# A layout change at the store side of a pairwise bilinear kernel: output rows 64 bytes longer in memory

## The chip, the cores and the metric

The kernel runs on one core of one Trainium2 chip. The metric is the device time of one launch in microseconds (us). Times of several runs are given as their median; a profile is one further execution, recorded by the hardware profiler, and its span runs from the first to the last instruction.

## The reference: what is computed

```python
# r_x: (4096, 32, 64) float32, W: (64, 64) float32
vid = jnp.einsum('bfd,de->bfe', x, W)
idx_i, idx_j = jnp.triu_indices(32, k=1)      # 496 pairs i < j
return x[:, idx_i, :] * vid[:, idx_j, :]      # (4096, 496, 64) float32
```

For each of 4096 samples, each of the 32 fields is multiplied by one 64x64 matrix, and then every pair of fields (i < j) gives one elementwise product. The input is 33.6 MB and the output 520 MB, so the kernel writes about fifteen times what it reads.

## The kernel before, in words

**Layout.** The host lays the input out transposed: 128 rows, one for each SBUF partition, where a row stands for one of the 64 embedding elements of one of two halves of the batch. Along a row, the data is cut into units of C = 128 float32 numbers, 512 B each: one unit holds one field (or one output pair) for 128 samples. The batch makes NT = 16 tiles of 256 samples (128 in each half). The output in memory is laid out in the same way, as 128 rows; each row holds 16 x 496 units of products, one tile after the other, and then PAD = 24 units that nobody writes or reads. A row is thus 7,960 units or 4,075,520 B long, which is 995 x 4,096 B. The host undoes this layout after the launch and drops the padding.

**Work.** For each tile, eight matmuls on TensorE (L172) multiply the 32 fields by a block-diagonal copy of W and leave `vid` in PSUM. VectorE then forms the 496 products with `tensor_tensor` (L196), reading x from SBUF and `vid` from PSUM by broadcast or strided views, in the order that `by_block` and `products` give. Everything in SBUF is one big tile `mem` of 445 units a partition. The products go into 70 slots in it, listed by hand in `SLOTS` with length and place, and the x tiles go to places listed in `XPLACE`, so that loads, products and stores share the memory as it comes free.

**Transfers.** All transfers are issued by SyncE (SP) in program order, and the order of SP and VectorE is the program's own. As soon as a slot is full, SP issues its store (L199): 128 partitions, and of each one a contiguous run of up to 127 units (65,024 B). The places in a row follow from `STARTS`: slot k is written to units `begin` to `end`, next to where slot k-1 ended. There are 70 stores. The 11 loads (L136, L140, L153) bring the first tile with W, then the other tiles in three groups. The first load of the program begins 256 B into a row of its array (`C - D` = 64 numbers), since W's 64 columns stand there.

The changed lines are the store at L199 and the host's declaration of the output array.

Of the kernel before, what the change touches and what calls it, by code (L numbers as in the profile page):

```python
# [14 lines left out]
C = 128  # L15
# [25 lines left out]


PAD = 24
PAD0 = 7


# [6 lines left out]
def by_block():  # L53


    def within(lo):
        yield "step", lo, 2, 1, 0
        for k in range(2):
            yield "step", lo, 4, 2, k
        for i in (lo, lo + 8):  # L60
            yield "row", i + 4, i, 4, 4
        yield "row", lo + 8, lo, 8, 8

    yield from within(0)
    yield "row", 16, 0, 16, 16
    yield from within(16)


def products(blocks, at=0):

    for kind, a, b, c, d in blocks:
        if kind == "row":
            rows, n, i0, di, j0, dj = c, d, b, 0, a, 1
        else:
            rows, n, i0, di, j0, dj = 16 // b, c, a, b, a + c + d, b
        r = k = 0
        while r < rows:
            room = BREAKS[bisect_right(BREAKS, at)] - at
            if k or room < n:
                m, w = 1, min(n - k, room)  # L80
            else:
                m, w = min(rows - r, room // n), n
            yield at, m, w, i0 + r * di + k, di, j0 + r * dj, dj
            at += m * w
            if k + w == n:
                r, k = r + m, 0
            else:
                k += w
# [10 lines left out]
@with_exitstack  # L99
def pairwise_bilinear_kernel(  # L100
    ctx: ExitStack,
    tc: tile.TileContext,
    x0: bass.AP,
    x: bass.AP,
    out: bass.AP,
):

    nc = tc.nc
    NT = sum(len(tiles) for group in GROUPS for tiles in group)
    F = x0.shape[1] - 1 - PAD0
    D = P // 2
    NP = F * (F - 1) // 2

    BANK = 512 // C


    ctx.enter_context(tc.manual_schedule(engines={mybir.EngineType.SP, mybir.EngineType.DVE}))

    const = ctx.enter_context(tc.tile_pool(name="const", bufs=1))
    psum = ctx.enter_context(
        tc.tile_pool(name="ps", bufs=1, space=bass.MemoryType.PSUM)
    )
    vid = psum.tile([P, F, C], F32)

    mem = const.tile([P, UNITS, C], F32)


    w2 = const.tile([P, P], F32)


    place = XPLACE[0]
    nc.sync.dma_start(  # L136
        out=mem.rearrange("p u c -> p (u c)")[:, place * C - D : (place + F // 2) * C],
        in_=x0.rearrange("p u c -> p (u c)")[:, C - D : (1 + F // 2) * C],
    )
    nc.sync.dma_start(out=mem[:, place + F // 2 : place + F, :], in_=x0[:, 1 + F // 2 : 1 + F, :])  # L140
    nc.vector.memset(w2, 0.0)  # L141
    for half in (slice(0, D), slice(D, P)):
        nc.vector.tensor_copy(w2[half, half], mem[half, place - 1, C - D :])  # L143
    loaded = 1

    def load(tiles, cuts=()):
        nonlocal loaded
        n = len(tiles) * F
        place = XPLACE[tiles[0]]
        at = (loaded - 1) * F  # L150
        loaded += len(tiles)
        return [
            nc.sync.dma_start(out=mem[:, place + lo : place + hi, :], in_=x[:, at + lo : at + hi, :])  # L153
            for lo, hi in cuts or [(0, n)]
        ]

    ready = mybir.DependencyInfo(mybir.DependencyClass.Sync, mybir.DependencyReason.DATA)

    def behind(later, earlier):
        tc.add_manual_dep(later.ins, earlier.ins.name, ready, reason="issued when that has landed")  # L160

    pieces = []
    groups, cuts = iter(GROUPS), iter(CUTS)
    for tiles, parts in zip(next(groups)[1:], next(cuts)):
        pieces = load(tiles, parts)

    for t in range(NT):
        xt = mem[:, XPLACE[t] : XPLACE[t] + F, :]


        for b in range(0, F, BANK):
            nc.tensor.matmul(  # L172
                vid[:, b : b + BANK, :],
                lhsT=w2,
                rhs=xt[:, b : b + BANK, :],
                start=True,
                stop=True,
            )

        for at, m, w, i, di, j, dj in products(by_block(), t * NP):  # L180
            slot = bisect_right(STARTS, at) - 1
            n = m * w
            begin, end = STARTS[slot], STARTS[slot + 1]
            ot = mem[:, SLOTS[slot][1] : SLOTS[slot][1] + SLOTS[slot][0], :]
            o = ot[:, at - begin : at - begin + n, :]
            if m == 1:
                left = xt[:, i : i + w, :]
                right = vid[:, j : j + 1, :].to_broadcast([P, w, C])
            else:
                o = o.rearrange("p (m w) c -> p m w c", m=m)  # L190
                right = vid[:, j : j + (m - 1) * dj + 1 : dj, :].unsqueeze(2).to_broadcast([P, m, w, C])
                if di == 0:
                    left = xt[:, i : i + w, :].unsqueeze(1).to_broadcast([P, m, w, C])
                else:
                    left = xt.rearrange("p (m d) c -> p m d c", d=di)[:, i // di : i // di + m, i % di : i % di + w, :]
            nc.vector.tensor_tensor(o, left, right, ALU.mult)  # L196
            at += n
            if at == end:
                store = nc.sync.dma_start(out=out[:, begin:end, :], in_=ot)  # L199
                if pieces:  # L200
                    behind(store, pieces[-2])
                    pieces.clear()


        if t + 2 == loaded < NT:
            (tiles,) = next(groups)
            pieces = load(tiles, next(cuts))
# [45 lines left out]
```

## Time and profile before

| | |
|---|---|
| median of 3 runs | 1287.49 us (1287.32 to 1287.50) |
| the profiled execution | 1287.45 us, of which the span is 1285.6 us |
| TensorE matmul busy | 230.2 us, 256 instructions |
| VectorE busy | 1084.0 us, 348 instructions |
| DMA, queue of the kernel's transfers | 11,664 packets, 553.69 MB, 99.8% of 16 engines' span |
| HBM read and written | 33.59 MB and 520.09 MB |

A packet is one record of a DMA engine: one contiguous run that it moved, or one semaphore update of 4 B at the end of its share of a transfer. 81 transfers of 128 rows make 10,368 runs, and 81 x 16 engines make 1,296 semaphore updates, which together are the 11,664 packets of the queue. The share of 16 engines' span says how much of the time the engines were occupied with packets. The trace holds each packet's start, duration and size.

### The profile page before, as it was taken

The numbers are of one execution on the slowest core, as the hardware profiler recorded it, in microseconds if no ns is written. First come the engines' busy times: TensorE is split into PE (matmuls) and PEld (weight loads), VectorE is DVE, ScalarE is ACT, GpSimd is POOL, SyncE is SP. The second block draws the span as 40 slices with busy tenths as digits, with TensorE's granted clock in tenths as the row PEclk, the third lists the DMA queues.
The fourth block names the chain that finished last, engine by engine and source line by source line (L and its number), as shares of the span: only waits on it lengthen the run. The fifth ranks groups of instructions, "written<-read, shape, count | busy, mean of one in ns | idle before, by whom it ended". The sixth has DMA issues, their size and how long they took to land.

```text
span 1285.6 us, 1143 instructions
## 1 busy us (share of the span) xinstructions
PE 230.2 (18%) x256; PEld 66.9 (5%) x256; DVE 1084.0 (84%) x348; POOL 0.2 (0%) x4
## 2 busy tenths in 40 slices
PE   4031221303120112040311211103122130312000
PEld 1000000100000000010000000000000000000000
DVE  6899998999967389899799992849998889999952
POOL 0000000000000000000000000000000000000000
PEclk8555565556555556555555555555556555555555
DMA  9999999999999999999999999999999999999998
GB/s 415 417 440 440 441 414 449 420 442 416 445 430 439 418 420 435 434 440 429 441 427 449 429 427 438 417 440 421 440 432 443 437 422 440 427 447 422 436 443 364
DMA packets 11670, 553.75 MB, mean 431 GB/s; under 512 B 1296, under 2 KB 1296, under 8 KB 1680
## 3 DMA queue, kind: packets, MB, share of 16 engines
q1 hardware_dynamic: 11664, 553.69, 99.8%
q8 instruction: 2, 0.03, 0.0%
q14 instruction: 4, 0.03, 0.0%
HBM read 33.59 MB, written 520.09 MB: 431 GB/s over the span
## 4 chain that ended last, share of the span: by engine, by line
DMA 46%; DVE 45%; issue 6%; DVEq 0%; SPq 0%
DVE mem L196 45%; DMA out_dram<-mem 41%; DMA mem<-in_r_x_dram 5%; DVEq L241 0%; SPq L153 0%; DVEq L196 0%; SPq L140 0%; SPq L136 0%; SPq L199 0%
## 5 line engine op out<-in xcount | busy, mean ns | idle before, releaser
L196 DVE TENSOR_TENSOR mem<-mem,vid 128x1024 f32<-128x1024 f32 (+17 forms) x345 | 1083.4, 3212 | 170.6 <-DMA out_dram<-mem 164.6
L172 PE MATMUL vid<-mem,w 128*128 128x512 f32 x256 | 230.2, 1034 | 952.8 <-DVE mem L196 885.0
L172 PEld LDWEIGHTS vid<-mem,w 128*128 128x128 f32 x256 | 66.9, 303 | 1114.5 <-DVE mem L196 1013.1
L143 DVE COPY w<-mem 64x64 f32<-64x64 f32 x2 | 0.4, 190 | 5.0 <-DMA mem<-in_r_x_dram 5.0
L141 DVE MEMSET w<- 128x128 f32 x1 | 0.2, 165 | 0.8 <-PEq L221 0.8
L221 POOL MEMSET const-bfloat16-1.0<- 128x1 bf16 x1 | 0.1, 101 | 0.0
L221 POOL MEMSET const-uint8-127<- 128x1 uint8 x1 | 0.1, 101 | 0.0
L221 POOL MEMSET const-float32-0.0<- 128x1 f32 x1 | 0.1, 98 | 0.2 <-issue 0.2
L221 POOL MEMSET const-float32-1.0<- 128x1 f32 x1 | 0.1, 98 | 0.0
## 6 DMA issues: line engine op xcount, KB each, us to landing
out_dram<-mem SPq DMA_DIRECT2D x15, 8128.0 KB, 27.5
out_dram<-mem SPq DMA_DIRECT2D x14, 7680.0 KB, 24.9
out_dram<-mem SPq DMA_DIRECT2D x6, 7168.0 KB, 26.2
out_dram<-mem SPq DMA_DIRECT2D x5, 7936.0 KB, 28.1
out_dram<-mem SPq DMA_DIRECT2D x3, 7424.0 KB, 22.6
out_dram<-mem SPq DMA_DIRECT2D x3, 5888.0 KB, 20.9
mem<-in_r_x_dram SPq DMA_DIRECT2D x2, 8128.0 KB, 37.9
out_dram<-mem SPq DMA_DIRECT2D x2, 8064.0 KB, 24.3
```

What stands on the lines that cost most here:

```text
L141: nc.vector.memset(w2, 0.0)
L143: nc.vector.tensor_copy(w2[half, half], mem[half, place - 1, C - D :])
L172: nc.tensor.matmul(vid[:, b : b + BANK, :], lhsT=w2, rhs=xt[:, b : b + BANK, :], start=True, stop=True,)
L196: nc.vector.tensor_tensor(o, left, right, ALU.mult)
L221: nc = _bacc.Bacc("TRN2", target_bir_lowering=False, num_devices=1, dynamic_dma_scratch_size=512)
```

## The change

Each row of the output in memory becomes 16 float32 numbers (`SHIFT`, 64 B) longer than before. Row p therefore begins 64 x p bytes later than it did. To allow a row length that isn't a whole number of units, the output is declared with two dimensions instead of three, and the store names its place in numbers instead of units. The loads, the products, the slots and the order of all instructions are as before: the instruction lists of the two programs have the same 70 stores of the same shapes, with the same waits, in the same places.

```diff
 PAD = 24
+SHIFT = 16
 PAD0 = 7
...
             if at == end:
-                store = nc.sync.dma_start(out=out[:, begin:end, :], in_=ot)
+                store = nc.sync.dma_start(out=out[:, begin * C : end * C], in_=ot.rearrange("p u c -> p (u c)"))
...
-        laid = (2 * D, NT * shape[1] + PAD, C)
+        laid = (2 * D, (NT * shape[1] + PAD) * C + SHIFT)
...
-    got = r.results[0]["out_0_dram"][:, : NT * NP].reshape(2, D, NT, NP, C)
+    got = r.results[0]["out_0_dram"][:, : NT * NP * C].reshape(2, D, NT, NP, C)
```

A row is now 4,075,584 B long. Before, every run of every store began and ended at a multiple of 512 B from the start of the array. Now 16 of the 128 rows (p a multiple of 8) still do; 32 (p a multiple of 4) begin at multiples of 256 B; 96 begin 64, 128 or 192 B past one. The SBUF side of each store is as it was.

## The prediction

> **What bounds the kernel now.** I read the engine table and the 40 slices first, then the queue table, then the waits of VectorE and of SP's queue, and then single packets. The first view is the page's engine line and its slices:
>
> ```profile
> PE 230.2 (18%) x256; PEld 66.9 (5%) x256; DVE 1084.0 (84%) x348; POOL 0.2 (0%) x4
> ...
> DMA  9999999999999999999999999999999999999998
> GB/s 415 417 440 440 441 414 449 420 442 416 445 430 439 418 420 435 434 440 429 441 427 449 429 427 438 417 440 421 440 432 443 437 422 440 427 447 422 436 443 364
> ```
>
> No compute engine fills the span, and the DMA digits stand at 9 in all slices but the last. The GB/s vary because a packet counts where it ends. The queue table says how full "9 or more" is:
>
> ```profile
> q1 hardware_dynamic: 11664, 553.69, 99.8%
> ...
> HBM read 33.59 MB, written 520.09 MB: 431 GB/s over the span
> ```
>
> The engines are occupied 99.8% of the span. The waits confirm who sets the pace. The two fences are the waits of VectorE and the waits of SP's queue (for what, us in total, times, longest):
>
> ```profile
> DVE mem L196 <- DMA out_dram<-mem: 164.6, 33, 21.6
> ```
>
> ```profile
> SPq L199 <- DVE mem L196: 1101.6, 66, 32.4
> ...
> SPq L241 <- DMA out_dram<-mem: 23.8, 1, 23.8
> ```
>
> VectorE is idle 164.6 us because a slot's old contents were still being stored. SP waits for VectorE too, 1101.6 us, but that starves nothing: a store takes 24.9 us (median) from issue to landing and 16 engines need about 17 us for its 7.43 MB (520.09 MB / 70 at 431 GB/s), so the next one is issued while the last one runs. In the packet records at least 16 packets are under way in 1275 of the 1285.6 us. The chain of waits changes hands between VectorE (45%) and the stores (41%), so neither view alone names a bound; what VectorE's 1084 us leave room for and the transfers don't decides it.
>
> So the time is the sum of the packets' durations over 16 engines, and a store packet's duration is the one thing that this change can touch. The steady part shows how regular they are (queue table of the stretch from 1000 to 1250 us):
>
> ```profile
> q1 hardware_dynamic: 1945, 108.40, 100.1%
> ```
>
> 108.40 MB in 1.001 x 16 x 250 us is 27.07 GB/s for one engine. The packet records say the same: the 65,024 B packets take 2399 ns in the median (2401.9 mean), the 61,440 B ones 2267 ns, the 8,192 B ones 309 ns, the 3,584 B ones 140 ns. A line through the first and the last of these is 27.20 GB/s plus 8.2 ns a packet. A semaphore update, 4 B, takes 9 ns.
>
> **The budget.** 553.7 MB / 16 engines / 27.20 GB/s is 1272.3 us. 10,368 / 16 = 648 runs an engine, at 8.2 ns, are 5.3 us. 81 updates an engine, at 9 ns, are 0.7 us. That makes 1278.3 us. All packet durations together, over 16, are 1282.9 us, so some 4.6 us lie above the line; 4.0 us of that are packets longer than the median of their own size. They come mostly where loads and stores run together: 62 KB stores that begin at 413 us take 2815 to 3342 ns instead of 2286 ns, and 13 KB loads after 440 us up to 1192 instead of 498. The other 2.7 us of the span are the start before the first packet and the end. Outside the span lie 1287.45 - 1285.6 = 1.85 us. The profiled execution is 0.04 us off the median of 1287.49 us, so its sum stands for the median.
>
> **The change part by part.** The declaration, the two-dimensional view and the host's slice change no instruction: 70 stores of the same shapes with the same waits, 256 matmuls and 345 products stay. I cost them at nothing, because a run is already the whole contiguous part of a row (65,024 B in one packet). If the two-dimensional view changed how a row is cut, the packet count of 11,664 would tell, and each additional cut would cost an engine 8.2 ns.
>
> Loads don't change either. What changes is the destination address of 8,960 store runs, 560 an engine. There are two effects to price.
>
> First, the odd start and end. A run that begins 64 B past a 256 B boundary has a short piece at its head and one at its tail. No operation of the trace before writes at such an address, so I bound it. From below: nothing, if the engine's pace is set on the SBUF side and short pieces are absorbed; the address on the SBUF side is unchanged. The nearest row for an offset is the first load, which begins 256 B into its row: its 8,448 B packets take 319 ns in the median, and the line gives 8448 / 27.20 + 8.2 = 318.8 ns. An offset of 256 B costs nothing, at least in reading, so I take the 32 of 128 rows on 256 B multiples as free and the other three quarters as touched: 420 runs an engine (if each engine gets its even share). The nearest row for a short write is the semaphore update, 9 ns. One more short piece a run is 420 x 9 ns = 3.8 us; two, head and tail, 7.6 us. The upper bound is a cut not only at the ends but inside. I take one piece, 3.8 us: the head must be written short, while the tail of one run and the head of the next store adjoin in memory and may overlap with the end-of-run cost that is already in the 8.2 ns.
>
> The Trainium skill, page "DMA: Bandwidth & Descriptors", section "How a descriptor splits into AXI transactions", speaks against this change: a descriptor that doesn't start on a 256 B boundary begins with a transaction from the boundary below, and the unused bytes still cost beats. An estimate from that page, up to 192 B unused, is one 256 B transaction more a run, and at the trace's 27.20 GB/s that is 9.4 ns and 4.0 us in all, or 1291.4 us. No packet before starts so, and the page describes reading, so no row confirms it for writes.
>
> Second, the pitch. Row starts were all at multiples of 4,096 B (995 of them apart); now row p lies 64 x p bytes further, so the engines, which work on different rows, no longer write the same place within a 4,096 B block at the same time. If memory conflicts among them cost anything now, it lies in the 4.0 us of long packets; the steady stretch after 1000 us has next to none (its packets are at their medians). The most that can be won is 4.0 us. In the other direction a new conflict could lengthen packets, but for the base case I take 0, because the memory keeps pace with 16 engines at 27.1 GB/s for hundreds of us.
>
> The same page, "Latency and other measured facts", has a row on pitches near 4 MiB: 103 GB/s at 4 MiB, 214 with 4 KiB added, 97 with 192 B added instead. By that ratio, 97 to 103, an estimate would be 1287.45 x 103 / 97 = 1367 us. This case's packets already run at 27.1 GB/s an engine, so the regime of that row isn't this one, and no run before shows a pitch with a small addition.
>
> Sum: 1287.45 + 3.8 + 0 = 1291.3 us. Nothing covers an added cost here, since engines hold packets throughout: VectorE's and SP's slack lies beside the transfers and takes none of it. A longer store only shifts work: VectorE's idle time of 164.6 us on stores would grow by about what the span grows.
>
> **The rivals.** *Nothing measurable* (1287.5 us, within 0.2%, which is 2.6 us and about what a measurement of this kernel can tell from no change): the pace is set where data leaves SBUF, and short pieces at the memory end are absorbed. For it speaks that one rate, 27.20 GB/s, fits packets of 3,584 to 65,024 B, loads and stores alike, so the memory's side doesn't seem to matter; against it, that the engine has no spare time in which to hide anything.
>
> *Faster, by spread rows*: the 64 B steps remove conflicts, and the long packets fall to their medians: 1287.45 - 4.0 = 1283.4 us. It decides when more than 2.6 of these 4.0 us go. For it: conflicts do exist around 413 us and 818 us. Against it: they stand where loads join, and the addition doesn't change the loads' addresses; stores by themselves are already at the line.
>
> *A cut all along the run*: source and destination are no longer aligned with each other, and every piece of some fixed size straddles a boundary, so it is written in two. Cuts each 4,096 B, priced at 9 ns, would be 58,046 / 4096 = 14 a mean run, 14 x 9 ns x 420 = 53 us, 1340 us; each 512 B eight times as much, some 1710 us. For it speaks only that no row shows a 64 B offset; against it, that an engine which streams 65 KB in one packet seems to need no boundary inside it. The two-dimensional view cutting rows anew would look like this as well, with more packets.
>
> **How the numbers follow.** Short pieces that show (2.6 to 10 us more): 0.40. Nothing measurable: 0.28. Faster: 0.12. A cut along the run, or another conflict of over 1%: 0.20. Slower is 0.40 + 0.20 = 0.60. The range begins at the faster rival's 1283.5 us. Its upper end takes in the two-piece bound (1295.1 us) and half of the 53 us for 4,096 B cuts, 1314 us, for a piece may well cost less than a packet of its own; what lies above is most of the 0.20. The likeliest case's own range is 1290 to 1297 us.
>
> **What would show it.** The page after should have 11,664 packets, 553.69 MB and 99.8% again, and VectorE's 1084 us. The step with the short pieces is right if the 65,024 B packets have a median about 9 ns longer (2408) in three of four rows and 2399 in the fourth. If all stay at 2399 and the time too, the absorbing rival holds; if the outliers at 413 and 818 us go, the spreading one. If packets grow in proportion to their size, it is the cut along the run, and my pricing by the ends is wrong. More VectorE waiting without longer packets would make the whole argument wrong.

## The result, and the profile after

The changed kernel takes 1289.20 us in the median of 20 runs (1288.62 to 1289.57), the kernel before 1287.33 us in 20 runs beside them (1286.83 to 1287.88). That is 1.87 us more, a ratio of 1.0014 with a 95% interval of 1.0008 to 1.0020: slower, but by less than the 0.2% that were called measurable, by half of the 3.8 us that were forecast, and below the 1290 to 1297 us of the likeliest case. The profiled execution took 1288.92 us against 1287.45 us.

The page of the changed kernel, its engine line, the DMA slices and the queue table (packets, MB, share of 16 engines' span):

```profile
span 1287.1 us, 1143 instructions
...
PE 228.6 (18%) x256; PEld 66.3 (5%) x256; DVE 1084.2 (84%) x348; POOL 0.2 (0%) x4
...
DMA  9999999999999999999999999999999999999998
...
q1 hardware_dynamic: 11664, 553.69, 99.7%
...
HBM read 33.59 MB, written 520.09 MB: 430 GB/s over the span
```

The same 11,664 packets and the same bytes, the same work on VectorE, engines as full as before, and a span 1.5 us longer. Nothing new waits. VectorE's wait for stores and SP's wait for VectorE (from the waits of VectorE and of SP's queue: us in total, times, longest) grew by 1.1 and 1.3 us, about the lengthening of the span:

```profile
DVE mem L197 <- DMA out_dram<-mem: 165.7, 33, 21.6
```

```profile
SPq L200 <- DVE mem L197: 1102.9, 66, 32.3
```

So the time went into the packets themselves. The queue table of one stretch, 850 to 1000 us, shows it, first before and then after:

```profile
q1 hardware_dynamic: 1423, 65.19, 100.4%
```

```profile
q1 hardware_dynamic: 1423, 65.00, 100.3%
```

A packet counts in the stretch in which it begins, with its whole duration, so a share can pass 100%. For one full share of the engines, that is 65.19 / 1.004 = 64.93 MB before and 65.00 / 1.003 = 64.81 MB after: 0.2% less moved in the same time. The single packet records are sharper. Give each run of over 20,000 B the time that the line of before gives (bytes at 27.198 GB/s plus 8.2 ns), and list what it took beyond it. These are eight runs of 65,024 B of one store on one engine, near 600 us, in ns beyond the line:

```
before:   0  0  0  0  0  0   0  0
after:    0  0  6  7  0  0  12  7
```

Fifteen of the sixteen engines show nearly only zeros there before. After, the same eight-run figures return on engine after engine, and other stores have other figures that return in the same way, so this isn't chance. But 100 to 380 us looked different already in the kernel before: there most engines had runs 2 to 24 ns beyond the line, and the change adds little to these. The mean of all runs by stretch, in ns beyond the line (stretches without loads; a stretch in which nearly all runs of before lie on the line is called quiet below):

| stretch, us | before | after | difference |
|---|---|---|---|
| 100 to 200 | 5.55 | 6.58 | 1.03 |
| 200 to 380 | 5.62 | 5.89 | 0.27 |
| 500 to 600 | 0.69 | 5.17 | 4.48 |
| 600 to 800 | 0.64 | 4.86 | 4.22 |
| 850 to 1000 | 0.53 | 4.91 | 4.38 |
| 1000 to 1250 | 1.79 | 5.10 | 3.31 |

Of 560 store runs an engine, 176 belong to the first 22 stores (issued before 390 us) and 384 to the rest. The last four rows of the table, weighted by their runs, have a difference of 4.0 ns. 384 x 4.0 ns = 1.5 us and 176 x some 0.5 ns = 0.1 us make 1.6 us, beside 1.47 us between the two profiled executions and 1.87 us between the medians.

That the sums lie so close is in part luck, since the table leaves out the stretches with loads. All packet durations together, over 16 engines, grew from 1282.94 to 1283.87 us, by 0.9 us only: by 1.3 us in 460 to 790 and 870 to 1250 us, by 0.1 us in 30 to 380 us, while around the loads (380 to 460 and 790 to 870 us) they fell by 0.5 us. The rest is that the engines don't finish together. Their last semaphore updates come at 1282.2 us in the mean and at 1284.5 us on the last engine before; at 1283.1 and 1285.8 us after. The launch ends with the last engine, which moved by 1.3 us. What remained open was which property of the new addresses costs these nanoseconds.

### The profile page after: what moved, and what is told of

Same layout as the page of the kernel before. It is cut to its first block, busy times and chain, and to the rows that moved or that the text cites. A ratio compares the mean times of both kernels' runs of the same rounds, so it can differ in the third digit from the quotient of the medians.

```text
span 1287.1 us, 1143 instructions
## 1 busy us (share of the span) xinstructions
PE 228.6 (18%) x256; PEld 66.3 (5%) x256; DVE 1084.2 (84%) x348; POOL 0.2 (0%) x4
## 3 DMA queue, kind: packets, MB, share of 16 engines
q1 hardware_dynamic: 11664, 553.69, 99.7%
## 4 chain that ended last, share of the span: by engine, by line
DMA 48%; DVE 44%; issue 6%; DVEq 0%; SPq 0%
DVE mem L197 44%; DMA out_dram<-mem 43%; DMA mem<-in_r_x_dram 5%; DVEq L242 0%; SPq L154 0%; DVEq L197 0%; SPq L141 0%; SPq L137 0%; SPq L200 0%
```

## The experiments

Two theories at first: the *ends* (a run that begins off a 256 B grid pays something fixed) and the *pitch* (rows are no longer a multiple of 4,096 B apart and collide in memory). In all kernels below the order of work is that of the changed kernel; diffs are against it. "Beyond the line" is the mean of the stretch from 500 to 600 us unless another is named. That stretch is quiet in the kernel before (0.69 ns) and in the aligned kernels below; elsewhere aligned kernels differ among themselves, so that from 1000 to 1250 us the first kernel of this series reads 4.41 ns, and the kernel before 1.79.

**Two dimensions, old row length.**

```diff
-SHIFT = 16
+SHIFT = 0
```

> The store and the output array are written with two dimensions as in the changed kernel, but a row is as long as before. Theory of the ends (a run that begins off a 256 B multiple costs some 5 ns more; 6 of 8 rows do in the changed kernel, whose 65,024 B packets have a mean of 2404.8 ns against 2401.9, and whose undisturbed engines show 4.1 ns more a run): 1287.3 us, packets of 65,024 B at 2399 in the median and three quarters of them at 2399. Theory of the pitch (rows that are no longer a multiple of 4,096 B apart collide in memory): also 1287.3 us. Only if the two-dimensional view itself costs would this be 1289.2 us.

Measured: 1287.58 us (11 runs), ratio to before 1.0002 (0.9993 to 1.0011); 0.68 ns beyond the line. No cost of the notation shows.

**Rows 512 B longer.**

```diff
-SHIFT = 16
+SHIFT = 128
```

> Rows 512 B longer instead of 64 B: every run begins on a 512 B multiple again, but rows are still not a multiple of 4,096 B apart. Theory of the ends: 1287.3 us, the 65,024 B packets at 2399 ns from the 5% to the 75% point. Theory of the pitch: 1289 us or more, with packets spread above 2399 as in the changed kernel (2402 median, 2406 at 75%).

Measured: 1287.55 us (11 runs), 1.0002 (0.9993 to 1.0011), 0.67 ns.

**Rows 256 B longer.**

```diff
-SHIFT = 16
+SHIFT = 64
```

> Rows 256 B longer: every second row begins on an odd multiple of 256 B. Theory of the ends with a grid of 256 B: 1287.3 us, packets at 2399. With a grid of 512 B: half of the rows pay 5 ns, 280 x 5 ns = 1.4 us at most, about 1288.5 us. Theory of the pitch: about 1289 us, as in the changed kernel.

Measured: 1287.56 us (11 runs), 1.0003 (0.9994 to 1.0012), 0.66 ns. Neither pitch is a multiple of 4,096 B, and neither shows a cost, in the time (within some 0.1%) or in the quiet stretch. Half of the rows here begin on odd multiples of 256 B, so the grid that matters isn't 512 B; since starts 128 B off pay (below), it is 256 B.

**Old row length, all rows starting 64 B in.**

```diff
-SHIFT = 16
+SHIFT = 0
+OFFSET = 16
...
-                store = nc.sync.dma_start(out=out[:, begin * C : end * C], in_=ot.rearrange("p u c -> p (u c)"))
+                store = nc.sync.dma_start(out=out[:, OFFSET + begin * C : OFFSET + end * C], in_=ot.rearrange("p u c -> p (u c)"))
```

The host takes its slice from `OFFSET` on.

> Rows as long as before, but each row's products begin 64 B after the row does, so that all 128 rows begin 64 B past a multiple of 4,096 B and none is aligned. Theory of the ends: all 8 rows of an engine pay instead of 6, 1.87 x 8 / 6 = 2.5 us, 1289.8 us, and hardly any 65,024 B packet is left at 2399 ns in the stretch where the kernel before has nearly all of them there. Theory of the pitch: 1287.3 us, since the distance of rows is as before.

Measured: 1290.66 us (7 runs), 1.0028 (1.0017 to 1.0039), 3.1 us above the first kernel of this series on the same chip; 7.60 ns beyond the line. The pitch is that of before, and yet the price is higher than the change's, since now all rows pay. The queue table of 850 to 1000 us, of the kernel with the old row length and then of this one:

```profile
q1 hardware_dynamic: 1423, 65.32, 100.6%
```

```profile
q1 hardware_dynamic: 1424, 65.06, 100.5%
```

For one full share that is 65.32 / 1.006 = 64.93 MB, as before the change, and 65.06 / 1.005 = 64.74 MB, 0.3% less. The pitch theory falls; the ends theory stands, with 7.60 - 0.68 = 6.9 ns a run. Its forecast of 1289.8 us was too low, since it scaled the change's 1.87 us by 8/6: the runs off the grid cost 4.48 x 8 / 6 = 6.0 ns each there and 6.9 ns here, and the last engine ends 3.4 us after the mean of the sixteen here (1287.4 and 1284.0 us), against 2.7 us there.

What about the end costs? I tried the size of the offset, then each end by itself. From the tail on, the diffs show only the two arguments of the store (`...` stands for what is as before), and all these kernels have `SHIFT = 0`.

**All rows starting 128 B, and 4 B, in** (`OFFSET = 32` and `OFFSET = 1`, otherwise as above).

> Rows as long as before, every row's products begin 128 B after the row does. Theory of whole blocks (a run pays for every 256 B block of memory that it touches, and off the grid it touches one block more, whatever the offset): the same as with 64 B, 6.5 ns a run on undisturbed engines and some 3.1 us in all, 1290.6 us. Theory of unused bytes at the head alone (the bytes between the boundary below and the start are paid for, 2.35 ns at 64 B): twice the price of 64 B.

> Every row's products begin 4 B after the row does. Theory of whole blocks: again 6.5 ns a run and 1290.6 us. Theory of unused bytes at the head alone: next to nothing, 1287.5 us. A third possibility is that starts off a multiple of 64 B cost more than all others because part of a memory word is written at each end: then tens of ns a run and 1300 us or more.

Measured: 1290.58 us (9 runs), 1.0026 (1.0016 to 1.0036), 7.59 ns beyond the line; and 1290.63 us (9 runs), 1.0026 (1.0016 to 1.0036), 7.61 ns. The same as at 64 B within 0.02 ns in the mean, and in the single figures: the same store reads 13 0 5 14 5 5 5 14 on engines of all three kernels. How far off the grid a run starts doesn't matter, not even down to 4 B; that it is off does. Paying for the unused bytes at the head falls, and so does a penalty for starts off 64 B.

**The tail alone off the grid.**

```diff
-SHIFT = 16
+SHIFT = 0
...
-...out=out[:, begin * C : end * C], in_=ot.rearrange("p u c -> p (u c)")...
+...out=out[:, begin * C : end * C - 16], in_=ot.rearrange("p u c -> p (u c)")[:, : (end - begin) * C - 16]...
```

> Every run begins where it does before the change, aligned, and leaves out its last 16 numbers (64 B), so that only its tail is off the grid. The largest runs are 64,960 B, which the line of 27.20 GB/s and 8.2 ns puts at 2396.6 ns. Theory of whole blocks: the run touches as many blocks as the full one, so 2399 ns stay and the time is 1287.5 us. Theory of the head: 2396.6 ns and 560 x 2.35 ns = 1.3 us less, 1286.2 us. If a short tail costs as a piece of its own, 9 ns: some 2405 ns and 1291 us.

**The head alone off the grid, in SBUF too.**

```diff
-...out=out[:, begin * C : end * C], in_=ot.rearrange("p u c -> p (u c)")...
+...out=out[:, begin * C + 16 : end * C], in_=ot.rearrange("p u c -> p (u c)")[:, 16:]...
```

> Every run leaves out its first 16 numbers, in SBUF as in memory: it begins 64 B past a 256 B multiple on both sides and ends aligned. Theory of whole blocks at the memory side: 2399 ns for 64,960 B and 1287.5 us, as for the tail. Theory of the head: 2396.6 + 6.5 = 2403 ns and some 1289.3 us. Theory of the relative position (what costs is that source and destination lie differently within a block, which they don't here nor in the tail's case): 2396.6 ns and 1286.2 us in both.

Measured: 1286.82 us (10 runs), 0.9996 (0.9986 to 1.0005), and 1286.89 us (10 runs), 0.9997 (0.9987 to 1.0006); both 0.75 ns beyond the line, with the 64,960 B runs at 2396 ns in most of the stretch. In a quiet stretch, neither a ragged tail (an end off the grid) nor a ragged head costs anything by itself. That refutes, for quiet stretches, whole blocks as I had put it (2399 ns would have stayed) and my own idea of a price for each short piece.

Elsewhere the saving is lost: from 200 to 380 us both kernels lie 8.1 to 8.2 ns beyond the line, some 2.5 ns above the kernel before, so a run 64 B shorter, which by the line saves 2.35 ns, takes about as long there as the full one. That fits the time, which fell by 0.5 to 0.6 us and not by the 1.3 us that the bytes are worth; a small price of a ragged end outside quiet stretches isn't excluded.

Two explanations for the price of runs of full length were left: the *relative position* of source and destination within a block, or *one block more*: a 65,024 B run fills 254 blocks of 256 B in SBUF and, off the grid, touches 255 in memory, while the shortened runs touch 254 on both sides.

**Source off the grid, destination on it; and the reverse.** Both runs are 64 B shorter, so that blocks are 254 to 254, but the two sides lie 64 B apart within a block.

```diff
-...out=out[:, begin * C : end * C], in_=ot.rearrange("p u c -> p (u c)")...
+...out=out[:, begin * C : end * C - 16], in_=ot.rearrange("p u c -> p (u c)")[:, 16:]...
```

> Each store reads its slot from 64 B on and writes it, 64 B shorter, to the aligned place in memory, so products land 64 B too early: the memory side begins on the grid, the SBUF side 64 B past it. Theory of the relative position (source and destination lie differently within a 256 B block, whichever of them is off): the price of the start at 64 B, some 6 ns a run on undisturbed engines, and with the bytes left out 1289.0 us. Theory of the block more (the price is for a run that touches one block more in memory than in SBUF; here both touch 254): as the tail and the head alone, 1286.8 us, with the stretch from 500 to 600 us at 2396 ns.

```diff
-...out=out[:, begin * C : end * C], in_=ot.rearrange("p u c -> p (u c)")...
+...out=out[:, begin * C + 16 : end * C], in_=ot.rearrange("p u c -> p (u c)")[:, : (end - begin) * C - 16]...
```

> Each store reads its slot from its aligned beginning, leaves out its last 64 B, and writes from 64 B past the aligned place, so that a run begins off the grid in memory and ends on it; products land 64 B too late. The number of blocks is again 254 on both sides for the largest runs. Theory of the relative position: 6 ns a run, 1289.0 us. Theory of the block more: 1286.8 us.

Measured: 1286.75 us (10 runs), 0.9995 (0.9986 to 1.0004), 0.75 ns; and 1286.67 us (10 runs), 0.9994 (0.9985 to 1.0004), 1.06 ns. The relative position costs nothing in the quiet stretch. In the last kernel every run begins 64 B past the grid in memory, as all of them do in the kernel of 1290.66 us, reads from the aligned place, and pays next to nothing; it differs in being 64 B shorter and ending on the grid. Its queue table of 850 to 1000 us shows it as well:

```profile
q1 hardware_dynamic: 1416, 65.01, 100.1%
```

65.01 / 1.001 = 64.95 MB, the amount of the aligned kernels. (Not all four shortened kernels are quiet from 850 to 1000 us: tail, head, source and this one read 0.58, 5.48, 2.72 and 1.28 ns, with figures in the second and third that don't return from engine to engine.) The times and the quiet stretch fit the additional block. They don't show it alone: every run that paid had both its ends off the grid in memory, and every run that didn't had at least one end on it. A run that is off at both ends and yet touches no more blocks than its bytes fill (128 B shorter, from 64 B past the grid to 64 B before it) would separate the two and wasn't tried. Nor do these runs tell whether memory is to be compared with the blocks that the bytes fill or with those touched in SBUF. "The additional block" below stands for this one condition, both ends off the grid at full length.

**Twice as many runs, aligned and at 64 B.** Each store is cut into two, without and with the offset of 16 numbers. The diff is that of the aligned halves; the second kernel adds 16 to every place in `out`, and the host's slice follows.

```diff
-                store = nc.sync.dma_start(out=out[:, begin * C : end * C], in_=ot.rearrange("p u c -> p (u c)"))
+                flat, cut = ot.rearrange("p u c -> p (u c)"), (end - begin) // 2 * C
+                nc.sync.dma_start(out=out[:, begin * C : begin * C + cut], in_=flat[:, :cut])
+                store = nc.sync.dma_start(out=out[:, begin * C + cut : end * C], in_=flat[:, cut:])
```

> Every store is issued as two, each half of the run, with all starts aligned; nothing is left out. All theories: 560 runs more an engine at 8.2 ns and 70 semaphore updates at 9 ns, 5.2 us more, 1292.7 us. It is the base for the next kernel.

> Every store is issued as two halves and every row's products begin 64 B after the row does, so that each of 1,120 runs an engine is off the grid. If the price belongs to the run, the step from the aligned halves is twice that from whole aligned runs to whole runs at 64 B, 2 x 3.1 = 6.2 us: 1298.9 us. If it belongs to the byte, the step stays at 3.1 us: 1295.8 us.

Measured: 1292.79 us (5 runs), 1.0043 (1.0029 to 1.0057), and 1299.84 us (4 runs), 1.0097 (1.0082 to 1.0112). The first lies 0.1 us from what the 8.2 ns a run and 9 ns an update gave, in part by luck, since the aligned halves lack what whole runs lose in the first 400 us (below). The step between them is 7.05 us, more than twice the 3.1 us of whole runs, which a price by the byte can't give. The queue table of 500 to 600 us, aligned halves first, then halves at 64 B:

```profile
q1 hardware_dynamic: 1826, 43.28, 100.4%
```

```profile
q1 hardware_dynamic: 1800, 42.87, 100.2%
```

Per full share that is 43.11 MB against 42.78 MB, 0.8% less. The packet records put the halves at 0.42 ns beyond the line and the halves at 64 B at 7.29 ns: 6.9 ns more, as for runs twice as long. So the price belongs to the run and not to the byte. The aligned halves run undisturbed from the start (0.27 ns beyond the line from 100 to 200 us, where the whole runs of before show 5.55 ns), and their offset version pays in full there (7.20 ns). But that isn't why the step exceeds 6.2 us. The last semaphore updates of the engines tell:

| kernel | mean of 16 engines, us | last engine, us |
|---|---|---|
| whole runs, aligned, two dimensions | 1282.24 | 1284.77 |
| whole runs, all at 64 B | 1283.96 | 1287.39 |
| halves, aligned | 1288.14 | 1289.48 |
| halves at 64 B | 1291.50 | 1296.59 |

In the mean the step is 1.7 us for whole runs and 3.4 us for halves, twice as much, as a price by the run should be. Both are below 560 or 1,120 x 6.9 ns, for packets around the loads get shorter at 64 B, as in the changed kernel. The other half of the 7.05 us is one engine that ends 5.1 us after the mean at 64 B, against 1.3 us aligned. Why one engine falls behind when runs are off the grid wasn't tried and stays open.

No experiment pointed to a kernel faster than the one before: aligned runs are the best of these cases, and the four that came out lower leave out 64 B of each run.

## Why the prediction was right or wrong

**The bound** held in kind: with all instructions and packets in place, the span moved with the packets, and VectorE's and SP's slack took none of it. But the sum over 16 engines is a mean, and the launch ends with the last engine, 2.3 us after the mean before and 2.7 us after. Of the 1.47 us between the profiled executions, the mean engine's packets account for 0.9 us.

**The term of the short piece** had the right form, a fixed price for each run off the grid, and was mis-sized: 420 runs x 9 ns = 3.8 us were forecast, 1.87 us measured. Two things failed in its size. The price came from the semaphore update's 9 ns as the nearest row; the runs showed 6.0 ns for a run off the grid in the changed kernel (4.48 ns over all rows, of which three quarters are off), and 6.9 ns where every row is off. And "nothing covers an added cost here" was wrong for the first 380 us, where runs were already 5.6 ns beyond the line in the kernel before and the change added only 0.3 to 1.0 ns; so 384 of the 560 runs an engine paid most of the price, and the others little. Around the loads, packets even got shorter by 0.5 us an engine. I had seen that the packets of one size don't all take their median, but put the remainder to loads and stores running together; by stretches it would have shown as two regimes. (The times 413, 440 and 818 us in the prediction are counted from the first packet record, some 11 us before the span begins; in the span's time they are about 402, 429 and 807 us. A packet counts where it begins, and not where it ends as the prediction has it.)

**The test set for it** was not met: three of four rows at 2408 ns and the fourth at 2399. The 65,024 B median moved by 3 ns (2402), not 9. Between 500 and 600 us 39% of the runs lie within 1.5 ns of the line after (96% before), more than a quarter, because the price doesn't fall on each run alike. Whether the rows on 256 B are the free ones can't be read off, since a packet record doesn't name its row; of the eight places in a store none reads 0 in every store.

**Where the head or the tail pays**: I argued that the head must be written short while the tail may hide. Neither pays alone in a quiet stretch, so the mechanism as predicted, a short piece written at the head, is wrong. A count that fits all runs is blocks touched in memory against those that the bytes need; that both ends must be off the grid fits them too.

**The grid of 256 B**, taken from the first load's 319 ns, was right for writes too (rows 256 B longer: no cost seen; starts 128 B off: the full price).

**The Trainium skill**, page "DMA: Bandwidth & Descriptors", section "How a descriptor splits into AXI transactions", gave 9.4 ns a run as an estimate. Its 256 B unit is the grid that the runs show, and where it has one transaction more for a full run, the runs show 6.0 to 6.9 ns. Its statement on unused bytes ahead of an unaligned start, which it makes of reading, isn't borne out for these stores: starts 4 B, 64 B and 128 B off cost the same in memory, and an unaligned source (the store that reads from 64 B on) cost nothing in the quiet stretch. The same page's row on pitches near 4 MiB, under "Latency and other measured facts", gave 6% as an estimate, from its figure with 192 B added; here, at a pitch that is no power of two, additions of 256 and 512 B showed no cost and 64 B cost 0.14%, by its ends and not by its pitch.

**The rivals.** *Nothing measurable* is where the time came to lie by size (0.14%, within the 0.2%), but not for its reason: packets did grow, and 20 runs of each told 0.14% from nothing. It had a chance of 0.28; the likeliest case, at 0.40, had the right sign and too high a price, and the stated range of 1283.5 to 1314 us was wide enough to hold both. *Spread rows* is refuted: the 62 KB stores that begin at 402 us still take up to 3324 ns (3342 before), and kernels with other pitches are no faster. Near 805 us the 62 KB stores did fall, from at most 3193 to 3033 ns, but with all rows at 64 B and the old pitch they fell further, to 2547 ns, so that isn't the spreading. *A cut all along the run* is refuted by the halves: the price doesn't grow with a run's length (6.9 ns for both).

## What to carry to other kernels

Where DMA engines are full for the whole span, count what each contiguous run costs beyond its bytes: here 8.2 ns for the run and 6 to 7 ns more if both its ends lie off the 256 B grid in memory. With runs of 58 KB that is 0.1 to 0.3% of the time; with runs of 29 KB it was already 0.5% (half of it one late engine), and for the same cost a run the share grows as runs get shorter. Row lengths and starts on multiples of 256 B avoided it at all three pitches tried. A price seen in a quiet stretch should be multiplied only by the runs in quiet stretches; and since the launch ends with the last engine, look at each engine's end beside the mean.

## What the runs showed of the hardware that I had not expected

The engines have two regimes at the same load. In the kernel before, most of them run 2 to 24 ns beyond the line a packet until the loads at 387 us, while between 500 and 1000 us 95 to 98% of the packets are within 1.5 ns of it, leaving out 800 to 850 us, where loads run. It isn't the pitch of the rows, since the kernels with rows 256 and 512 B longer show it alike (5.67 and 5.71 ns from 200 to 380 us, against 5.62); and the aligned halves have no such first stretch (0.80 ns there). Nor does it belong to the beginning: from 1000 to 1250 us the share within 1.5 ns is 81% before and 44 to 64% in the three aligned kernels of whole runs. What starts and ends this regime wasn't tried and stays open. In it, most of the additional block is absorbed: with all rows at 64 B, runs lie 6.9 to 7.8 ns beyond the line in every stretch of the table above, so the first stretch is hardly dearer than the quiet ones.

The price of the additional block comes unevenly: 6.9 ns in the mean, but in single runs mostly 0, 3 to 5, 9 or 13 to 14 ns (all rows at 64 B) in a fixed order that returns with the store. Why a block that would take 256 B / 27.2 GB/s = 9.4 ns by its size costs 6.9 ns in the mean was not settled.
